# Pairwise bilinear interaction: embedding depth on the partitions, six large stores per tile of 256 rows, each input tile loaded in quarters

## The chip, the cores and the metric

The kernel runs on one core of one Trainium2 chip. The metric is the device time of one execution in microseconds, the median of several runs. The transpositions of arrays on the host, before and after the launch, are not in this time.

## What is computed

The input `x` has 4096 rows (the batch), 32 fields per row and 64 numbers per field, in float32. `W` is a 64 x 64 matrix. Every field is multiplied by `W`, and then, for each of the 496 pairs of fields i < j, the left field is multiplied element by element with the projected right field:

```python
vid = jnp.einsum('bfd,de->bfe', x, W)
idx_i, idx_j = jnp.triu_indices(32, k=1)
return x[:, idx_i, :] * vid[:, idx_j, :]        # (4096, 496, 64)
```

The pairs are ordered by i, then by j: field 0 has the first 31 pairs, field 1 the next 30, field 30 the last one. The output is 520 MB, the input 34 MB.

## The kernel before

The batch lies on the partitions: a tile is 128 rows, one row per partition, and there are 32 tiles. For each tile:

- **Load** (line 61): one DMA of 1 MB from the SP queue. There are three buffers. The tile's load is issued two tiles ahead (lines 64 and 76; `AHEAD = 2`), before the stores of the tile that is then worked on.
- **Transposes** (line 85): the projection contracts over the depth, so the depth must be on the partitions. TensorE transposes two fields at a time, 16 transposes of 128 x 128 per tile, four to a PSUM bank; ScalarE copies each bank to `xT` in SBUF (line 86).
- **Projection** (line 97): 31 small matmuls per tile, one for each field but field 0 (the profile counts two matmul instructions for each), with `xT` of one field as the stationary side and `W` as the moving side (64 columns). The even fields of the pairs lie on partitions 0 to 63, the odd ones on 64 to 127, so `W` is loaded twice (lines 68 and 69, from ScalarE's queue). ScalarE copies the products from PSUM to `vid` (line 106), two buffers.
- **Products** (line 117): VectorE has one instruction for each left field i. It multiplies field i, broadcast along the pairs, with fields i+1 to 31 of `vid`, and writes 31-i pairs (of 64 numbers) to an output tile.
- **Stores** (line 124): consecutive left fields are gathered until they hold at most 66 pairs (`CHUNK`); each such chunk is one store from the SP queue. There are nine stores per tile, of 0.9 to 2.1 MB, from six output buffers.

Waits between engines and DMAs are put in by the tile framework: a consumer waits for the producers of what it reads, and a writer of a buffer waits until its earlier users are through. The order on each engine's queue is that of the program, planned by the framework's scheduler, which may move an instruction by its priority. On SP stand only loads and stores: a store there waits for VectorE's products, and everything behind it on SP waits with it.

Line 142 of the profile's rows is where the kernel's core object is made, and line 151 is the launch; neither does work on the data.

Of the kernel before, what the change touches and what calls it, by code (L numbers as in the profile page):

```python
# [1 line left out]

# [5 lines left out]

F32 = mybir.dt.float32
ALU = mybir.AluOpType  # L10


def field_chunks(nf, most):
    """Consecutive left fields i whose pairs (i, j > i) make one store of at most `most` pairs."""
    chunks, cur, size = [], [], 0
    for i in range(nf - 1):
        n = nf - 1 - i
        if cur and size + n > most:
            chunks.append((cur, size))
            cur, size = [], 0  # L20
        cur.append(i)
        size += n
    chunks.append((cur, size))
    return chunks


@with_exitstack
def pairwise_bilinear_kernel(
    ctx: ExitStack,
    tc: tile.TileContext,  # L30
    x: bass.AP,
    w: bass.AP,
    out: bass.AP,
):
    nc = tc.nc
    P = 128
    B, F, D = x.shape
    NT = B // P
    # Two fields (2 * D = 128 columns) share one transpose; 4 transposes fill a
    # PSUM bank, and so do the products of 8 fields.  # L40
    TPB = 4
    GRP = 8
    NGRP = F // (2 * GRP)
    CHUNK = 66
    AHEAD = 2

    const = ctx.enter_context(tc.tile_pool(name="const", bufs=1))
    xpool = ctx.enter_context(tc.tile_pool(name="x", bufs=AHEAD + 1))
    tpool = ctx.enter_context(tc.tile_pool(name="xT", bufs=2))
    vpool = ctx.enter_context(tc.tile_pool(name="vid", bufs=2))  # L50
    opool = ctx.enter_context(tc.tile_pool(name="out", bufs=6))
    ps_t = ctx.enter_context(
        tc.tile_pool(name="ps_t", bufs=3, space=bass.MemoryType.PSUM)
    )
    ps_v = ctx.enter_context(
        tc.tile_pool(name="ps_v", bufs=2, space=bass.MemoryType.PSUM)
    )

    def load(t):
        xt = xpool.tile([P, F, D], F32, tag="x", name=f"x_{t}")  # L60
        nc.sync.dma_start(out=xt, in_=x[t * P : (t + 1) * P])
        return xt

    loaded = [load(t) for t in range(min(AHEAD, NT))]

    # W on both halves of the partitions, for the even and the odd field of a pair.
    w2 = const.tile([P, D], F32)
    nc.scalar.dma_start(out=w2[0:D, :], in_=w)
    nc.scalar.dma_start(out=w2[D : 2 * D, :], in_=w)
    ident = const.tile([P, P], F32)  # L70
    make_identity(nc, ident)

    chunks = field_chunks(F, CHUNK)
    for t in range(NT):
        if t + AHEAD < NT:
            loaded.append(load(t + AHEAD))
        xt = loaded[t]

        # xT[(parity, d), pair, b] = x[b, 2 * pair + parity, d]
        xT = tpool.tile([P, F // 2, P], F32, tag="xT", name=f"xT_{t}")  # L80
        for g in range(F // 2 // TPB):
            pt = ps_t.tile([P, TPB, P], F32, tag="pt", name=f"pt_{t}_{g}")
            for k in range(TPB):
                f = 2 * (g * TPB + k)
                nc.tensor.transpose(pt[:, k, :], xt[:, f : f + 2, :], ident)  # L85
            nc.scalar.copy(xT[:, g * TPB : (g + 1) * TPB, :], pt)  # L86

        # vid[b, j] = x[b, j] @ W. Field 0 is never the right one of a pair.
        vid = vpool.tile([P, F // 2, 2, D], F32, tag="vid", name=f"vid_{t}")
        for g in range(NGRP):  # L90
            pv = ps_v.tile([P, 2, GRP, D], F32, tag="pv", name=f"pv_{t}_{g}")
            for k in range(GRP):
                pair = g * GRP + k
                for h in range(2):
                    if pair == 0 and h == 0:
                        continue
                    nc.tensor.matmul(  # L97
                        pv[:, h, k, :],
                        lhsT=xT[h * D : (h + 1) * D, pair, :],
                        rhs=w2[h * D : (h + 1) * D, :],  # L100
                        start=True,
                        stop=True,
                    )
            for h in range(2):
                k0 = 1 if g == 0 and h == 0 else 0
                nc.scalar.copy(  # L106
                    vid[:, g * GRP + k0 : (g + 1) * GRP, h, :], pv[:, h, k0:, :]
                )
        vid = vid.rearrange("p g h e -> p (g h) e")

        start = 0
        for c, (fields, size) in enumerate(chunks):
            ot = opool.tile([P, CHUNK, D], F32, tag="o", name=f"o_{t}_{c}")
            at = 0
            for i in fields:
                n = F - 1 - i
                nc.vector.tensor_tensor(  # L117
                    ot[:, at : at + n, :],
                    xt[:, i : i + 1, :].to_broadcast([P, n, D]),
                    vid[:, i + 1 :, :],  # L120
                    ALU.mult,
                )
                at += n
            nc.sync.dma_start(
                out=out[t * P : (t + 1) * P, start : start + size, :],
                in_=ot[:, :size, :],
            )
            start += size


_INS = ["r_x", "L0_rec_W"]
_OUTS = [((4096, 496, 64), "float32")]


# [21 lines left out]
```

## Time and profile before

| | |
|---|---|
| median of 9 runs | 1331.4 us (1328.48 to 1336.02) |
| the profiled execution's own time | 1336.02 us |
| its span in the profile | 1334.2 us |
| bytes read from and written to HBM | 33.59 and 520.09 MB, 415 GB/s over the span |
| VectorE busy | 1142.1 us (86%), 992 instructions |
| TensorE busy | 257.6 us (19%), 2496 matmul and transpose instructions |
| ScalarE busy | 139.3 us (10%), 257 instructions |
| granted TensorE clock, mean | 0.566 |

A group's row in the profile reads: line, engine, operation, output <- inputs, shapes, how often; then the busy time in us and the mean duration of one in ns; then how long the engine stood idle just before these instructions, and what ended most of that idle time. The DMA row gives, for each of 40 equal slices of the span, the mean busy share of the 16 DMA engines in tenths; the row under it gives the GB/s that they moved. A row of DMA issues gives the operands, the queue (SPq is SyncE's), how often, the size, and the median time from issue to landing. The profile's chain is the work that ended last, followed back from the end to whatever released each step.

### The profile page before, as it was taken

The page shows a single profiled execution, that of the slowest core. Times are in us where ns is not written, and L with a number is a line of the kernel's source. Part 1 is how long each engine was busy: PE and PEld are TensorE (multiplying, and loading weights), DVE is VectorE, ACT ScalarE, POOL GpSimd, SP SyncE. Part 2 cuts the span into 40 slices and gives each one's busy share as a digit, 9 for nine tenths or more (in the row PEclk, how much of TensorE's full clock was granted, in tenths as well). Part 3 has the DMA queues.
Part 4 walks back from the last instruction along what each step waited for, and adds up shares of the span by engine and source line. Part 5 has one row for each costly group of instructions (what it writes and reads, how often), then busy time and mean ns, then how long its engine had stood idle before and what let it go on. Part 6 is the DMA issues. An engine that isn't in the chain of part 4 may idle for free.

```text
span 1334.2 us, 7305 instructions
## 1 busy us (share of the span) xinstructions
PE 257.6 (19%) x2496; PEld 244.5 (18%) x2496; DVE 1142.1 (86%) x992; ACT 139.3 (10%) x257; POOL 0.7 (0%) x6
## 2 busy tenths in 40 slices
PE   5012221222212332102222022220122311322000
PEld 5012221122211332102222022220122311322000
DVE  5999888888888888889888888888898888988893
ACT  3011101011010110101101011100111010110000
POOL 0000000000000000000000000000000000000000
PEclk9566665566655556556665566665666555566555
DMA  6999999999999999999999999999999999999996
GB/s 271 404 428 429 427 422 425 421 429 423 421 421 425 425 428 426 420 427 428 427 427 419 421 421 416 426 421 420 419 418 429 420 418 425 411 427 418 421 428 282
DMA packets 46277, 554.16 MB, mean 415 GB/s; under 512 B 5280, under 2 KB 5280, under 8 KB 9376
## 3 DMA queue, kind: packets, MB, share of 16 engines
q1 hardware_dynamic: 46080, 553.67, 98.8%
q8 instruction: 19, 0.31, 0.1%
q14 instruction: 18, 0.15, 0.0%
q10 hardware_dynamic: 160, 0.03, 0.0%
HBM read 33.59 MB, written 520.09 MB: 415 GB/s over the span
## 4 chain that ended last, share of the span: by engine, by line
DMA 75%; DVE 21%; issue 2%; PE 1%; DVEq 0%; ACT 0%
DMA out_dram<-o 75%; DVE o L117 21%; DMA x<-in_r_x_dram 0%; PE pv L97 0%; PE pt L85 0%; DVEq L117 0%; ACT vid L106 0%; DVEq L151 0%
## 5 line engine op out<-in xcount | busy, mean ns | idle before, releaser
L117 DVE TENSOR_TENSOR o<-x,vid 128x1984 f32<-128x1984 f32 (+30 forms) x992 | 1142.1, 1220 | 171.3 <-DMA out_dram<-o 156.8
L85 PE MATMUL pt<-ident,x 128*128 128x128 f32 x512 | 111.6, 408 | 970.4 <-DMA x<-in_r_x_dram 970.0
L85 PEld LDWEIGHTS pt<-ident,x 128*128 128x128 f32 x512 | 100.9, 220 | 974.4 <-issue 973.4
L86 ACT COPY xT<-pt 128x512 f32<-128x512 f32 x128 | 74.1, 588 | 711.4 <-PE pt L85 711.0
L97 PE MATMUL pv<-w,xT 64*128 64x64 f32 x1984 | 148.4, 311 | 0.0
L97 PEld LDWEIGHTS pv<-w,xT 64*128 64x128 f32 x1984 | 143.6, 224 | 8.9 <-issue 8.9
L106 ACT COPY vid<-pv 128x512 f32<-128x512 f32 (+1 forms) x128 | 64.2, 586 | 385.6 <-DVE o L117 381.4
L86 ACT ACT_TABLE_LOAD x1 | 1.3, 1283 | 2.0 <-issue 2.0
masks.py:199 POOL TENSOR_SCALAR_AFFINE_SELECT ident<-ident 128x128 f32<-128x128 f32 x1 | 0.3, 292 | 0.1
masks.py:197 POOL MEMSET ident<- 128x128 f32 x1 | 0.2, 204 | 0.3 <-POOLq L142 0.3
L142 POOL MEMSET const-bfloat16-1.0<- 128x1 bf16 x1 | 0.1, 101 | 0.0
L142 POOL MEMSET const-uint8-127<- 128x1 uint8 x1 | 0.1, 101 | 0.0
L142 POOL MEMSET const-float32-0.0<- 128x1 f32 x1 | 0.1, 98 | 0.2 <-issue 0.2
L142 POOL MEMSET const-float32-1.0<- 128x1 f32 x1 | 0.1, 98 | 0.0
## 6 DMA issues: line engine op xcount, KB each, us to landing
out_dram<-o SPq DMA_DIRECT2D x64, 1824.0 KB, 23.3
out_dram<-o SPq DMA_DIRECT2D x32, 2112.0 KB, 22.5
out_dram<-o SPq DMA_DIRECT2D x32, 2016.0 KB, 21.7
out_dram<-o SPq DMA_DIRECT2D x32, 1984.0 KB, 21.5
out_dram<-o SPq DMA_DIRECT2D x32, 1952.0 KB, 24.6
out_dram<-o SPq DMA_DIRECT2D x32, 1696.0 KB, 24.2
out_dram<-o SPq DMA_DIRECT2D x32, 1568.0 KB, 23.5
x<-in_r_x_dram SPq DMA_DIRECT2D x32, 1024.0 KB, 24.5
```

The source lines that it names most:

```text
L85: nc.tensor.transpose(pt[:, k, :], xt[:, f : f + 2, :], ident)
L86: nc.scalar.copy(xT[:, g * TPB : (g + 1) * TPB, :], pt)
L97: nc.tensor.matmul(pv[:, h, k, :], lhsT=xT[h * D : (h + 1) * D, pair, :], rhs=w2[h * D : (h + 1) * D, :], start=True, stop=True,)
L106: nc.scalar.copy(vid[:, g * GRP + k0 : (g + 1) * GRP, h, :], pv[:, h, k0:, :])
L117: nc.vector.tensor_tensor(ot[:, at : at + n, :], xt[:, i : i + 1, :].to_broadcast([P, n, D]), vid[:, i + 1 :, :], ALU.mult,)
L142: nc = _bacc.Bacc("TRN2", target_bir_lowering=False, num_devices=1)
```

## The change

The host hands the kernel another layout, and takes the output back in another. The batch is cut in two halves of 2048 rows. A tile is now 256 rows, 128 from each half, and there are 16 tiles. Partitions 0 to 63 hold the 64 depths of the first half's rows, partitions 64 to 127 those of the second half's; along the free dimension lie 32 fields x 128 rows. The output is laid out in the same way, 496 pairs x 128 rows per partition. In the kernel:

- The transposes, their copies and the identity go. A matmul now has `W` as its stationary side and four fields (512 columns) as its moving side, one for each half of the partitions: 16 matmuls per tile of 256 rows, in four groups of 8 fields, each group in two PSUM banks and followed by one copy of 1024 columns on ScalarE. Field 0 is projected too.
- A product instruction works on fields of 128 numbers instead of 64. Pairs are stored in slots of 83 (`SLOT`), six slots per tile, the last of 81; a left field that crosses a slot's end is cut in two instructions. There are three output buffers.
- SP's instructions are issued in the order in which the program writes them (`manual_schedule` for SP).
- Input buffers: two instead of three. Tile 0 is loaded in four quarters (8 fields each), the last fields first, then tile 1 in two halves; both at the start. The quarters of every later tile t+1 are issued on SP behind the second, third, fourth and fifth of the six stores of tile t, fields 0 to 7 first.
- Tile 0 is worked from its last pair backwards and stored in smaller pieces (four stores for the first slot, two for each other slot), and its groups are projected in reverse.

```diff
-    TPB = 4
     GRP = 8
-    NGRP = F // (2 * GRP)
-    CHUNK = 66
+    NGRP = F // GRP
+    BANK = 512 // C
+    SLOT = 83
     AHEAD = 2
+    PIECES = 4
...
+    ctx.enter_context(tc.manual_schedule(engines={mybir.EngineType.SP}))
...
-    xpool = ctx.enter_context(tc.tile_pool(name="x", bufs=AHEAD + 1))
-    tpool = ctx.enter_context(tc.tile_pool(name="xT", bufs=2))
+    xpool = ctx.enter_context(tc.tile_pool(name="x", bufs=AHEAD))
     vpool = ctx.enter_context(tc.tile_pool(name="vid", bufs=2))
-    opool = ctx.enter_context(tc.tile_pool(name="out", bufs=6))
+    opool = ctx.enter_context(tc.tile_pool(name="out", bufs=3))
...
+    def load(t, lo, hi):
+        if t not in xs:
+            xs[t] = xpool.tile([P, F, C], F32, tag="x", name=f"x_{t}")
+        nc.sync.dma_start(out=xs[t][:, lo:hi, :], in_=x[t][:, lo:hi, :])
...
+        vid = vpool.tile([P, F, C], F32, tag="vid", name=f"vid_{t}")
+        for g in order:
+            pv = psum.tile([P, GRP, C], F32, tag="pv", name=f"pv_{t}_{g}")
+            for b in range(0, GRP, BANK):
+                f = g * GRP + b
                 for h in range(2):
+                    half = slice(h * D, (h + 1) * D)
                     nc.tensor.matmul(
+                        pv[half, b : b + BANK, :],
+                        lhsT=w2[half, :],
+                        rhs=xs[t][half, f : f + BANK, :],
                         start=True,
                         stop=True,
                     )
+            nc.scalar.copy(vid[:, g * GRP : (g + 1) * GRP, :], pv)
...
+    def products(t, vid, ot, base, a, b, backwards=False):
+        fields = [i for i in range(F - 1) if off[i] < b and off[i + 1] > a]
+        for i in reversed(fields) if backwards else fields:
+            s, e = max(a, off[i]), min(b, off[i + 1])
+            j = i + 1 + s - off[i]
+            nc.vector.tensor_tensor(
+                ot[:, s - base : e - base, :],
+                xs[t][:, i : i + 1, :].to_broadcast([P, e - s, C]),
+                vid[:, j : j + e - s, :],
+                ALU.mult,
             )
...
+    def store(t, ot, base, a, b):
+        nc.sync.dma_start(out=out[t][:, a:b, :], in_=ot[:, a - base : b - base, :])
+
+    for g in reversed(range(NGRP)):
+        load(0, g * GRP, (g + 1) * GRP)
+    load(1, F // 2, F)
+    load(1, 0, F // 2)
+
+    for t in range(NT):
+        vid = project(t, reversed(range(NGRP)) if t == 0 else range(NGRP))
+        bases = list(range(0, NP, SLOT))
+        if t == 0:
+            ends = [NP, off[27], off[24], off[21], bases[-1]]
+            for n, base in enumerate(reversed(bases)):
+                top = min(base + SLOT, NP)
+                if n:
+                    ends = [top, (base + top) // 2, base]
+                ot = opool.tile([P, SLOT, C], F32, tag="o", name=f"o_{t}_{n}")
+                for b, a in zip(ends, ends[1:]):
+                    products(t, vid, ot, base, a, b, backwards=True)
+                    store(t, ot, base, a, b)
+        else:
+            for n, base in enumerate(bases):
+                top = min(base + SLOT, NP)
+                ot = opool.tile([P, SLOT, C], F32, tag="o", name=f"o_{t}_{n}")
+                products(t, vid, ot, base, base, top)
+                store(t, ot, base, base, top)
+                if 1 <= n <= PIECES and t + 1 < NT and t + 1 not in (0, 1):
+                    load(t + 1, (n - 1) * F // PIECES, n * F // PIECES)
```

`off[i]` is the number of pairs ahead of left field i. `C` is 128, `NP` is 496.

## The prediction

> **What bounds the kernel now.** I read the page from its DMA row downwards, then the chain, then the product, matmul and issue rows, and last the trace at the two ends.
>
> ```profile
> span 1334.2 us, 7305 instructions
> ...
> DMA  6999999999999999999999999999999999999996
> GB/s 271 404 428 429 427 422 425 421 429 423 421 421 425 425 428 426 420 427 428 427 427 419 421 421 416 426 421 420 419 418 429 420 418 425 411 427 418 421 428 282
> ...
> q1 hardware_dynamic: 46080, 553.67, 98.8%
> ...
> DMA out_dram<-o 75%; DVE o L117 21%; DMA x<-in_r_x_dram 0%; PE pv L97 0%; PE pt L85 0%; DVEq L117 0%; ACT vid L106 0%; DVEq L151 0%
> ...
> L117 DVE TENSOR_TENSOR o<-x,vid 128x1984 f32<-128x1984 f32 (+30 forms) x992 | 1142.1, 1220 | 171.3 <-DMA out_dram<-o 156.8
> ...
> out_dram<-o SPq DMA_DIRECT2D x32, 1984.0 KB, 21.5
> out_dram<-o SPq DMA_DIRECT2D x32, 1952.0 KB, 24.6
> ...
> x<-in_r_x_dram SPq DMA_DIRECT2D x32, 1024.0 KB, 24.5
> ```
>
> The DMA row stands at 9 in 38 of 40 slices, and the chain is mostly stores: the kernel is bound by 553.67 MB of transfers, nearly all stores. VectorE is busy 1142.1 us and waits 156.8 us for output buffers, so it is only 14% short of being the bound itself. The load row matters most below: a load takes 24.5 us to land, because five or six stores stand ahead of it on the same queue. It costs nothing now, as it is issued two tiles (82 us) ahead.
>
> ```profile
> L117 DVE TENSOR_TENSOR o<-x,vid 128x1984 f32<-128x1984 f32 x32 | 71.2, 2225 | 35.3 <-DMA out_dram<-o 20.8 <-ACT vid L106 14.5
> ...
> L117 DVE TENSOR_TENSOR o<-x,vid 128x64 f32<-128x64 f32 x32 | 7.0, 218 | 0.0
> ```
>
> Those are two product rows by shape (busy us, mean ns). Next four lines of the timeline (start, us, engine, line): the matmuls of three tiles' projections, 62 instructions each for 31 products, and one load's issue in mid-run, which took 23.9 us to land.
>
> ```profile
> 9.44 3.90 PE L97 MATMUL pv<-w,xT 64*128 64x64 f32 x62
> ...
> 358.19 3.78 PE L97 MATMUL pv<-w,xT 64*128 64x64 f32 x62
> ...
> 441.31 7.09 PE L97 MATMUL pv<-w,xT 64*128 64x64 f32 x62
> ...
> 619.53 1.14 SPq L61 DMA_DIRECT2D x<-in_r_x_dram  x1
> ```
>
> Finer windows show first bytes at 1.5 us, full rate from 2.6 to 10.0 us (loads), nothing until 19.4 us (first store), and last bytes at 1332.7 us, 1.5 us before the span's end. **Pace:** 553.67 MB / (1332.7 - 2.6 - 9.4) = 419, say 420 GB/s.
>
> **What the Trainium skill says.** *DMA: Bandwidth & Descriptors*, "Queues, rings and completion order": each DMA engine consumes descriptors in ring order, one ring per engine for SP. The trace agrees: loads land after 24.5 us, stores after 21.5 to 24.6. *VectorE: DVE Perf Modes*, "The perf-mode tier table": fp32 tensor_tensor runs only at 1x. The trace agrees: (2225-218)/(1984-64) = 1.045 ns an element. *FP8 and Floating Point Precision*, "TensorE Precision Notes": an fp32 matmul makes four passes. The trace agrees: the burst at granted clock 0.50 (7.09 us) takes 229 ns a product, 274 cycles of 1.2 GHz for 64 columns. *TensorEngine Tiling (Array Packing)*, "Key Properties": tiles on different rows of the array work in parallel. No run here shows it: 274 cycles fit halves that take turns (4 x 64), but also parallel halves held up by their weights (128 columns, two instructions).
>
> **The change, part by part.** Bytes stay: a tile of 256 rows is 32.51 MB of stores and 2.10 MB of loads. A slot of 83 pairs stores 5.439 MB (12.95 us at 420), the last of 81 pairs 5.308 MB (12.64), a load quarter 0.524 MB (1.25).
>
> *VectorE.* Elements stay at 1,015,808 per partition: 1061.5 us at 1.045; the other 80.6 us of busy time are 81 ns for each of 992 instructions. After: 36 instructions a tile (31 fields, five cut at slot ends), so 63488 x 1.045 + 36 x 81 ns = 69.3 us a tile. The first slot (3 instructions) takes 11.35 us. Saving 416 instructions (34 us) brings nothing by itself: the transfers cover it.
>
> *Transposes and their copies* (111.6 us PE, 74.1 us ACT) go. They lay beside the stores in all tiles but the first: worth nothing there.
>
> *Start.* VectorE begins at 14.48 us now: load, transposes (3.65 us), matmuls, copies. After, it needs a quarter load, W (5.7 us from issue at 0.74, so 6.5), 4 matmuls (2.0 at the full clock that the trace shows here) and a copy (1.05): 9.7 us.
>
> *Matmuls.* Four of 512 columns per group of 8 fields. A matmul is 4 x 512 cycles. At half clock, halves in parallel, a group takes 2 x 2048 / 1.2 GHz + 0.2 = 3.6 us, an estimate from the two pages and the burst at clock 0.50. Bounds: 1.9 (full clock) and 7.0 (half clock, halves in turn). I take half clock, because PE stands idle some 14 us between quarters, and the parallel halves of the tiling page: the weights are loaded for only 64 columns now, so they hold up less. **Copy:** 588 ns for 512 columns, 0.83-1.1 ns a column more: 1.05 us for 1024.
>
> *Loads: the step that decides.* Before, a tile is loaded two tiles ahead. After, tile t+1's quarters are issued behind stores 2 to 5 of tile t's six, on the same SP queue. SP waits for each store's products first. Every pair's right field is above its left, so every first-slot product of t+1 needs the last quarter (fields 24-31). The quarter's own issue (1.1 us of SP's time in the load's row, four a tile) hides in the 11 us between two stores; it passes no other queue. Its wait for the x buffer (two now, three before) is over: tile t-1's products ended before the first store of t. So there is a loop that closes once a tile:
> - first slot's products 11.35, issue to first byte 0.7 (18.80 to 19.5 for the first store);
> - then the queue, back to back: 5 stores + 4 quarters = 29.29 MB / 420 = 69.74;
> - last byte to release 0.75 (the first store: 6.2 us to landing less 0.7 and 4.76 of transfer), PE start 0.13, matmuls 3.6, copy 1.05, VectorE start 0.1.
>
> Sum **87.4 us**, where the transfers alone need 82.4. Only the sixth store (12.64 us) lies behind the last quarter and covers its way back to a new store: 0.75+0.13+3.6+1.05+0.1+11.35+0.7 = 17.7. DMA idles 5.0 us a tile. VectorE's products plus latency alone (12.8) exceed the cover. Deeper buffers don't help: three slots of 12.95 never hold VectorE back within a tile (slot 3 would start 34 us in, the first store is through after 26).
>
> *Sum.* Tile 0, stored in pieces from the back: VectorE ends its first slot at 21.6 (81 x 128 x 1.045 + 13 x 81 ns), the next half slot at 27.5; from 28.2 on transfers bound it: 27.20 MB more, to 92.95. VectorE is through at 79.8. Tile 1's first store is ready at 91.85, no gap. Tile 2 starts at 92.95 + 69.74 + 5.63 = 168.3; tile 15 after 13 loops at 1304.8; its stores end 11.35 + 0.7 + 77.4 later: 1394.3, +1.5 = **span 1395.8**. Outside the span lie 1336.0 - 1334.2 = 1.8: 1397.6 against the profiled execution's 1336.0, +4.6%. The runs' median, 1331.4, is 0.34% below that execution; so 1393.
>
> *Descriptors.* 46080 packets are 320 DMAs x (128 rows + 16). After: 166 DMAs, rows of 42 KB. If all time in excess of the DMA page's fabric ceiling of 435 GB/s ("Specifications") goes with packets, 48 us fall to 25 and the pace becomes 427; if none does, it stays 420. The longer row pitch of the output could also slow it (lowest slice: 411). I take 420.
>
> **Rivals.**
> (a) *The loop, but a better pace:* 427 GB/s gives a loop of 86.3 and, by the same sum, 1374. For: half the packets. Against: at the start, loads in rows of 8 KB ran no slower (427 to 434 GB/s) than stores in rows of up to 17 KB.
> (b) *The matmul's halves take turns:* 7.0 for 3.6, 14 tiles: +48, 1440. For: 274 cycles. Against: the tiling page.
> (c) *No gap, faster:* the last quarter is not held up behind the fifth store. It decides at 11.9 us: if quarter, matmuls and copy are done within the last slot's products, the queue never empties; then 92.95 + 15 x 77.4 + 14 x 4.99 + 1.5 + 1.8 = 1327, as a median 1323. For: the quarters are small and 16 engines serve the queue. Against: 24.5 us of the load row.
> (d) *VectorE becomes the bound:* 16 x 69.3 = 1109; nothing speaks for it.
>
> **How the numbers follow.** Loop as priced 0.46, (a) 0.18, (b) 0.22: slower, 0.86. (c) 0.12: faster. 0.02 that pace and waits cancel. Some 0.2% is what a measurement of this kernel can tell from no change. Range: low 1350 = (a) with full-clock matmuls (-25), high 1445 = (b) and a little for its rounding; (c) and 0.06 beyond are left out.
>
> **What would show it.** Right: 14 waits of VectorE of some 18 us for ACT's copy, at the starts of tiles 2 to 15; DMA row below 9 about once in 87 us; last quarter landing some 20 us or more after issue; first slot's three products 11.35 us. Wrong: quarters landing within 12 us, VectorE waiting for stores instead, or a mid-run rate well above 430 GB/s.

## The result, and the profile after

The changed kernel takes **1415.1 us** in the median of 10 runs (1412.5 to 1418.5), the kernel before 1330.5 us in 32 runs. The ratio is **1.063** (95% interval 1.061 to 1.065): slower, by 6.3%, where 4.6% were forecast (1393 us, range 1350 to 1445). The profiled execution has a span of 1411.5 us, where the prediction's sum had 1395.8.

The page of the changed kernel, the lines that answer to those shown of before:

```profile
span 1411.5 us, 2185 instructions
...
DVE  6999397694986949859498594985949959499594
...
DMA  8999989899797997989989899798998989989799
GB/s 338 429 428 416 409 344 429 345 412 431 327 432 341 415 430 332 431 353 408 429 336 429 359 409 430 334 426 344 414 430 348 412 357 411 430 352 409 341 443 401
...
q1 hardware_dynamic: 23904, 553.66, 92.9%
...
DVE o L88 57%; DMA x<-in_r_x_dram 26%; PE pv L72 4%; ACT vid L79 1%; SPq L96 0%; DMA w<-in_L_rec_W_dram 0%; DVEq L154 0%
...
L88 DVE TENSOR_TENSOR o<-x,vid 128x1408 f32<-128x1408 f32 (+15 forms) x581 | 1099.4, 1973 | 292.0 <-ACT vid L79 292.0
...
x<-in_r_x_dram SPq DMA_DIRECT2D x60, 512.0 KB, 21.0
```

The bytes are the same, but the DMA row no longer stands at 9: every two or three slices it falls to 7 or 8, and the GB/s under it from 430 to about 340. The chain has changed hands. Before, three quarters of it were stores; now it is products, then loads, then matmuls and copies, in turn: a chain that goes round. VectorE no longer waits for output buffers at all; all its 292.0 us of waiting are for ScalarE's copies into `vid`.

One turn of the chain, in order of time (start us, duration us, what), from the issue of the fifth store to the next tile's first product:

```profile
494.44 0.33 SPq L96
...
494.82 26.17 DMA x<-in_r_x_dram
...
521.12 3.69 PE pv L72 x8
...
524.84 1.02 ACT vid L79
...
525.88 0.04 DVE o L88
```

SP issues the fifth store, then at once the last quarter. That quarter takes 26.17 us to land, since it stands behind what is left of the fourth store, the third quarter and the whole fifth store. Then come the four matmuls (eight instructions, 3.69 us), the copy and the release of VectorE. In the windows that follow (columns: stretch and its length, busy time of PE, PEld, DVE, ACT and POOL, granted clock, DMA share, GB/s) the queue runs dry. A window counts a row of a transfer where it starts, and a row of these stores takes about 1.6 us:

```profile
526.00:530.00 4.00, 0.00 (x0) 0.00 (x0) 4.00 (x1) 0.00 (x0) 0.00 (x0) 0.50 1.01 435
530.00:532.00 2.00, 0.00 (x0) 0.00 (x0) 2.00 (x2) 0.00 (x0) 0.00 (x0) 0.50 0.39 166
532.00:537.90 5.90, 0.00 (x0) 0.00 (x0) 5.90 (x3) 0.00 (x0) 0.00 (x0) 0.50 0.00 0
538.00:542.00 4.00, 0.00 (x0) 0.00 (x0) 4.00 (x3) 0.00 (x0) 0.00 (x0) 0.50 1.19 510
```

The sixth store, issued at 506.1, lands 27.1 us later, at about 533. VectorE works all the time on the next tile's first slot, but the store of that slot is issued only at 537.3, and its first bytes move at 538. For some 5 us nothing is on the way, as much as the prediction's sum had. VectorE's timeline shows the period (start, length of the run of instructions, first shape, how many, and in brackets the wait before it):

```profile
171.06 68.70 DVE L88 TENSOR_TENSOR o<-x,vid 128x3968 f32<-128x3968 f32 x36 [21.91 <-ACT vid L79]
259.83 68.70 DVE L88 TENSOR_TENSOR o<-x,vid 128x3968 f32<-128x3968 f32 x36 [20.07 <-ACT vid L79]
...
1322.71 68.70 DVE L88 TENSOR_TENSOR o<-x,vid 128x3968 f32<-128x3968 f32 x36 [20.20 <-ACT vid L79]
```

There are 14 such waits of about 20 us, at tiles 2 to 15. A tile takes (1322.71 - 171.06)/13 = **88.6 us**; forecast were 87.4.

### The profile page after: what moved, and what is told of

Read it like the earlier page. It is cut to its first block, busy times and chain, and to the rows that moved or that the text cites. A ratio compares the mean times of both kernels' runs of the same rounds, so it can differ in the third digit from the quotient of the medians.

```text
span 1411.5 us, 2185 instructions
## 1 busy us (share of the span) xinstructions
PE 221.9 (16%) x512; PEld 56.8 (4%) x512; DVE 1099.4 (78%) x581; ACT 66.1 (5%) x65; POOL 0.2 (0%) x4
## 4 chain that ended last, share of the span: by engine, by line
DVE 57%; DMA 27%; issue 9%; PE 4%; ACT 1%; SPq 0%; DVEq 0%
DVE o L88 57%; DMA x<-in_r_x_dram 26%; PE pv L72 4%; ACT vid L79 1%; SPq L96 0%; DMA w<-in_L_rec_W_dram 0%; DVEq L154 0%
## 5 line engine op out<-in xcount | busy, mean ns | idle before, releaser
L88 DVE TENSOR_TENSOR o<-x,vid 128x1408 f32<-128x1408 f32 (+15 forms) x581 | 1099.4, 1973 | 292.0 <-ACT vid L79 292.0
L72 PE MATMUL pv<-x,w 64*64 64x512 f32 x512 | 221.9, 1012 | 1099.8 <-DMA x<-in_r_x_dram 1094.4
L79 ACT COPY vid<-pv 128x1024 f32<-128x1024 f32 x64 | 64.8, 1012 | 1254.7 <-PE pv L72 1254.7
L72 PEld LDWEIGHTS pv<-x,w 64*64 64x64 f32 x512 | 56.8, 206 | 1263.1 <-issue 1252.3
```

What stands on the lines that cost most here:

```text
L72: nc.tensor.matmul(pv[half, b : b + BANK, :], lhsT=w2[half, :], rhs=xs[t][half, f : f + BANK, :], start=True, stop=True,)
L79: nc.scalar.copy(vid[:, g * GRP : (g + 1) * GRP, :], pv)
L88: nc.vector.tensor_tensor(ot[:, s - base : e - base, :], xs[t][:, i : i + 1, :].to_broadcast([P, e - s, C]), vid[:, j : j + e - s, :], ALU ...
```

## The experiments

**Theory:** the last quarter's place behind the fifth store closes a loop once a tile, with one store as cover, and the queue runs dry in each turn. **Rivals:** (1) the transfers themselves are slower in the new layout; (2) three output buffers are too few for stores of 5.4 MB; (3) TensorE's work is off the path and doesn't matter. Ratios are to the kernel before, run on the same chip beside each.

### Quarters one store earlier

```diff
-                if 1 <= n <= PIECES and t + 1 < NT and t + 1 not in (0, 1):
-                    load(t + 1, (n - 1) * F // PIECES, n * F // PIECES)
+                if n < PIECES and t + 1 < NT and t + 1 not in (0, 1):
+                    load(t + 1, n * F // PIECES, (n + 1) * F // PIECES)
```

> The four quarters of tile t+1 stand behind stores 1 to 4 of tile t instead of 2 to 5; nothing else differs. Theory (the once-a-tile loop: last quarter behind the fifth store, only the sixth store as cover): two stores (some 25 us) now cover a way of about 17.5 us, the queue never empties, VectorE's waits for ScalarE's copy at tile starts go, and a tile takes what its transfers take. In the trace of the changed kernel six stores take 74.7 us at 435 GB/s and a quarter some 2.05 us, so 82.9 us a tile instead of 88.6: span about 1332 us, ratio to the kernel before 1.00 (0.99 to 1.01). Rival 1 (the changed kernel is slow because its transfers are slow: other row sizes and another row pitch): the time stays near 1411. Rival 2 (three output buffers are too few for such large stores): also near 1411, with VectorE waiting for stores.

Measured: 1341.3 us, ratio 1.007 (1.005 to 1.009). Moving four loads by one store takes 74 us off. The page of this run:

```profile
DMA  8999999999999999999999999999999999999997
...
L88 DVE TENSOR_TENSOR o<-x,vid 128x1408 f32<-128x1408 f32 (+15 forms) x581 | 1101.7, 1971 | 212.7 <-ACT vid L79 135.2
...
410.00:420.00 10.00, 0.00 (x0) 0.00 (x0) 10.00 (x4) 0.00 (x0) 0.00 (x0) 0.54 0.79 341
```

The DMA row is back at 9 in all slices but the first and the last, and a tile takes 83.7 us (82.9 expected). VectorE still waits 135 us for ScalarE's copy, 9 us at the start of each tile, but that is within what VectorE has to spare in a tile (83.7 us, of which it works 68.7). Rivals 1 and 2 fall as explanations of the gap.

The queue is not quite full, though: the last line above is a window of this run at the turn of a tile, with a DMA share of 0.79. The trace has the landing of a transfer on each of the 16 DMA engines, and in this run three of them are some 7 us behind. Of the store issued at 430.98, for instance, 13 engines are done by 449.1, the last three at 453.4, 455.0 and 456.3. So 12 or 13 engines run dry for about 2 us before a tile's first store, while three or four always have work; the slowest set the pace of 83.7 us. In the changed kernel, whose queue runs empty in each tile, all 16 are done with a store at nearly the same time (the fifth one of the turn above: 518.0 to 519.3). Why three fall behind, these runs do not show.

### Quarters one store later

```diff
-                if 1 <= n <= PIECES and t + 1 < NT and t + 1 not in (0, 1):
-                    load(t + 1, (n - 1) * F // PIECES, n * F // PIECES)
+                if 2 <= n <= PIECES + 1 and t + 1 < NT and t + 1 not in (0, 1):
+                    load(t + 1, (n - 2) * F // PIECES, (n - 1) * F // PIECES)
```

> The quarters stand behind stores 3 to 6: no store is left behind the last quarter. Loop theory: a tile takes 11.3 + 0.8 (first slot's products, first byte) + 74.7 + 8.2 (six stores, four quarters) + 0.75 + 4.9 (release, matmuls, copy) = 100.7 us instead of 88.6: the span grows by 14 x 12.1 = 169 us to about 1580, ratio 1.19. Rivals 1 and 2 (slow transfers, too few output buffers): no change from the changed kernel, ratio 1.063.

Measured: 1580.2 us, ratio 1.185 (1.181 to 1.188), a span of 1574.7. VectorE's timeline of this run:

```profile
182.50 68.69 DVE L88 TENSOR_TENSOR o<-x,vid 128x3968 f32<-128x3968 f32 x36 [33.10 <-ACT vid L79]
...
1485.86 68.69 DVE L88 TENSOR_TENSOR o<-x,vid 128x3968 f32<-128x3968 f32 x36 [31.70 <-ACT vid L79]
```

A tile takes 100.3 us (expected 100.7). With one, two and no stores behind the last quarter the same bytes take 1415, 1341 and 1580 us.

### The last group's matmuls twice

```diff
-            for b in range(0, GRP, BANK):
+            for b in list(range(0, GRP, BANK)) * (2 if t > 1 and g == NGRP - 1 else 1):
```

> The changed kernel, but from tile 2 on the four matmuls of the last group of fields (24 to 31) are done twice, into the same place. Loop theory: TensorE's time for this group (3.7 us) is on the loop, so 14 x 3.7 = 51 us are added: span about 1463, ratio 1.10. If TensorE is beside the path (it is busy for 16% of the span), the time stays at ratio 1.063.

Measured: 1446.6 us, ratio 1.085 (1.082 to 1.088), a span of 1444.1: 33 us more, where 51 were expected. Two groups in this run's timeline:

```profile
514.82 3.68 PE L72 MATMUL pv<-x,w 64*64 64x512 f32 x8 [10.81 <-DMA x<-in_r_x_dram]
528.83 6.36 PE L72 MATMUL pv<-x,w 64*64 64x512 f32 x16 [10.33 <-DMA x<-in_r_x_dram]
```

Twice the work took 2.68 us more here, not 3.68: the longer burst ended faster (granted clock 0.50 in its first 5 us, 0.81 in its last 1.4). The 14 doubled bursts took 5.0 to 6.6 us, 5.9 in the mean, so 2.2 us more each: 14 x 2.2 = 31, nearly all of the 33. So the place on the path is confirmed, and rival 3 falls: an engine that is busy for 16% of the span is on the path with its last 3.7 us of every tile. The expectation's error was to charge the repetition at the pace of the first half.

### The whole load behind the first store, and four quarters together

```diff
-                if 1 <= n <= PIECES and t + 1 < NT and t + 1 not in (0, 1):
-                    load(t + 1, (n - 1) * F // PIECES, n * F // PIECES)
+                if n == 0 and t + 1 < NT and t + 1 not in (0, 1):
+                    load(t + 1, 0, F)                                      # first run
+                    for k in range(PIECES):                                # second run, in place of it
+                        load(t + 1, k * F // PIECES, (k + 1) * F // PIECES)
```

> Tile t+1 is loaded by one DMA of 2 MB behind store 1 of tile t. The loop predicts no idle queue, as with the quarters one store earlier. What this tells apart is the price of a quarter: in the changed kernel's trace four quarters seem to take some 8.2 us in the queue, 3.4 us more than their bytes at 435 GB/s. If each change from stores to a load and back costs (about 0.85 us), one load a tile instead of four saves 3 x 0.85 us x 14 tiles = 36 us against the quarters one store earlier: about 1296. If rows of 4 KB instead of 16 KB are what costs, the same gain is expected, so this run alone doesn't part these two. If neither costs, both runs come out alike.

> The same four quarter loads (rows of 4 KB) as in the changed kernel, but all four behind store 1, back to back. The runs before gave 1341 us for four quarters behind four stores and 1311 us for one load of 2 MB behind one store: a tile takes 83.75 and 81.2 us, that is about 0.87 us more than the bytes' time for every stretch of loads. If the change between stores and a load is what costs, four quarters together are one stretch: about 1311 us. If the rows of 4 KB are what costs, 1341 as with the quarters apart.

Measured: 1310.9 us, ratio 0.983 (0.980 to 0.985), for the whole load; 1301.6 us, ratio **0.978** (0.976 to 0.980), for the four quarters together. The latter is the fastest kernel of this study. VectorE's timeline of it, in one tile:

```profile
152.18 11.36 DVE L88 TENSOR_TENSOR o<-x,vid 128x3968 f32<-128x3968 f32 x3 [0.84 <-DMA out_dram<-o]
164.62 11.43 DVE L88 TENSOR_TENSOR o<-x,vid 128x896 f32<-128x896 f32 x4 [1.07 <-DMA out_dram<-o]
...
207.25 11.57 DVE L88 TENSOR_TENSOR o<-x,vid 128x1408 f32<-128x1408 f32 x6 [6.33 <-DMA out_dram<-o]
219.76 11.78 DVE L88 TENSOR_TENSOR o<-x,vid 128x384 f32<-128x384 f32 x13 [0.94 <-DMA out_dram<-o]
232.33 11.36 DVE L88 TENSOR_TENSOR o<-x,vid 128x3968 f32<-128x3968 f32 x3 [0.79 <-DMA out_dram<-o]
```

VectorE now waits for output buffers about 1 us a slot, the sign that the transfers are the bound, and 6.3 us where the loads are in the queue. A tile takes 80.5 us, with the quarters apart 83.7. The same four DMAs, with the same rows of 4 KB, cost 3.2 us less a tile when they stand together: it is the stretches of loads between stores that cost, about 1 us for each of the three that go away, and not the rows of 4 KB. That is the cost on the slowest engines. Added up over all 16, the pages have the transfers at 97.7% of 1340.6 us with the quarters apart and at 99.5% of 1299.4 us together, 17 us more and not 40; nearly all the rest is time in which most engines had run dry while the slow ones worked. What happens inside the DMA engines at such a change, these runs do not show.

### The first slot stored in thirds, then all slots

```diff
-                products(t, vid, ot, base, base, top)
-                store(t, ot, base, base, top)
+                for a, b in ((0, 28), (28, 56), (56, top)) if n == 0 else ((base, top),):       # first run
+                for a, b in ((base, base + 28), (base + 28, base + 56), (base + 56, top)):     # second run
+                    products(t, vid, ot, base, a, b)
+                    store(t, ot, base, a, b)
```

> The changed kernel with its quarters where they are, but from tile 1 on the first slot's store is cut into three (28, 28 and 27 pairs, each stored when its products are done). Loop theory: the products of the first slot are on the loop with their 11.35 us; with 28 pairs the first new store is ready after 3.8 us, so the way from the last quarter's last byte to a new store is 0.75 + 4.9 + 3.8 + 0.8 = 10.2 us, less than the 12.2 us of the sixth store: no empty queue, 83.75 us a tile as with the quarters one store earlier, about 1343 us, ratio 1.01. If the moment at which the load is issued is the trouble for another reason (the matmuls, the buffers), the time stays near 1415.

Measured: 1398.9 us, ratio 1.050 (1.048 to 1.053). That is 16 us less than the changed kernel and not the 70 expected. The windows of one tile (its first products start at 608.89) tell why:

```profile
622.00:626.00 4.00, 0.00 (x0) 0.00 (x0) 4.00 (x2) 0.00 (x0) 0.00 (x0) 0.50 1.03 436
626.00:630.00 4.00, 0.00 (x0) 0.00 (x0) 4.00 (x2) 0.00 (x0) 0.00 (x0) 0.50 0.08 35
630.00:634.00 4.00, 0.00 (x0) 0.00 (x0) 4.00 (x3) 0.00 (x0) 0.00 (x0) 0.50 0.40 170
```

The queue no longer runs dry before the first slot's store, but 17 us into the tile, before the second slot's: VectorE gains only about 1 us on the transfers in a slot (11.4 against 12.5), so a store that goes out early doesn't bring the next one forward. The gap had moved. The expectation had followed the loop only as far as the first store. If that is so, all slots must be cut:

> The changed kernel, quarters where they are, but from tile 1 on every slot's store is cut into three (28, 28 and 27 pairs), not the first slot's alone. With the first slot alone cut, the queue ran empty after its three pieces instead, since the second slot's products take 11.4 us and only 12.5 us of stores were ahead: the time fell by 16 us, not by 70. If that is the reason, cutting all of them keeps the queue fed: VectorE makes 28 pairs in 3.8 us, their store takes 4.2, and the first slot's 11.35 us on the loop become 3.8. The loop is then 3.8 + 0.8 + 63.2 (27.2 MB at 430) + 8.2 to 9 + 5.65 = 82 us, below the 84.9 us that a tile's transfers take (81.6 in the run with rows of 14 KB and quarters together, and 3.3 more for quarters apart): about 1316 + 14 x 3.3 = 1362 us, ratio 1.023 (1.015 to 1.035). If the first slot's products are not what the loop consists of, the time stays above 1395.

Measured: 1351.7 us, ratio 1.016 (1.013 to 1.018); the page's DMA row is at 9 in all slices but the first. A tile takes 84.2 us (84.9 expected), although VectorE still waits 14 to 15 us for ScalarE's copy at each start. So the gap has two cures: earlier loads, or smaller stores throughout. Both leave most DMA engines idle for some 2 us a tile, since the slowest are behind the others here too.

### Quarters on ScalarE's queue

```diff
-                    load(t + 1, (n - 1) * F // PIECES, n * F // PIECES)
+                    lo, hi = (n - 1) * F // PIECES, n * F // PIECES
+                    if t + 1 not in xs:
+                        xs[t + 1] = xpool.tile([P, F, C], F32, tag="x", name=f"x_{t + 1}")
+                    nc.scalar.copy(xs[t + 1][:, lo, 0:1], ot[:, top - base - 1, 0:1])
+                    nc.scalar.dma_start(out=xs[t + 1][:, lo:hi, :], in_=x[t + 1][:, lo:hi, :])
```

> The quarters are issued from ScalarE's queue instead of SP's, at the same moments as in the changed kernel: a one-column copy on ScalarE from the last pair of the slot into the quarter holds each load back until the slot's products are done (the column is then overwritten by the load). Loop theory in the form that the place in SP's ring is what counts: on a ring of its own a quarter takes turns with the stores on each DMA engine, 8 rows against 8 rows of a store, so it lands some 13 us after issue instead of 26; the last quarter, the matmuls and the copy are then through about 76 us after the tile's start, which is within the time of its transfers, and the time falls to that of the quarters one store earlier, about 1341, or somewhat more if the alternation costs. If it is the moment of issue that counts and not the ring (a load waits for all older stores whatever its queue), nothing changes: 1415, ratio 1.063.

Measured: 1571.0 us, ratio 1.181 (1.178 to 1.183). The run did not do what it was meant to. Its timeline:

```profile
621.67 3.68 PE L72 MATMUL pv<-x,w 64*64 64x512 f32 x8 [40.66 <-DMA x<-in_r_x_dram]
...
625.38 1.01 ACT L79 COPY vid<-pv 128x1024 f32<-128x1024 f32 x1 [20.36 <-PE pv L72]
626.29 0.19 ACT L128 COPY x<-o 128x1 f32<-128x1 f32 x1
626.51 0.33 ACTq L129 DMA_DIRECT2D x<-in_r_x_dram  x1
```

On ScalarE's queue the copy of one group of `vid` had been planned ahead of the next quarter's issue. So each quarter was issued only when the one before had landed and been projected, and the last of this tile went out at 672.8 us, 9 us before the next tile's first product. Here the DMA that was moved to a working engine's queue waited for that engine's own waits too. With ScalarE's instructions in the order of the program, too:

```diff
-    ctx.enter_context(tc.manual_schedule(engines={mybir.EngineType.SP}))
+    ctx.enter_context(tc.manual_schedule(engines={mybir.EngineType.SP, mybir.EngineType.Activation}))
```

> The quarters on ScalarE's queue again, with the same one-column copies that hold each back to the moment of the changed kernel, but ScalarE's instructions in the order of the program too: in the run before, the copies of one group stood ahead of the next quarter's issue on ScalarE, and so each quarter waited for the projection of the one before it. There a quarter landed 16.6 to 18.4 us after issue beside stores, against 26 in the changed kernel. So: last quarter issued 57.4 us after the tile's start, landed at about 75, projected and copied at 80: less than the 83.75 us of a tile's transfers, so no or nearly no empty queue and about 1340 us (1320 to 1360), ratio 1.01. If a ring of its own doesn't help, 1415; if alternation by rows slows both streams, between.

Measured: 1382.7 us, ratio 1.038 (1.036 to 1.041): between the two expectations. The last quarter's way, in this run's timeline:

```profile
656.64 0.33 ACTq L129 DMA_DIRECT2D x<-in_r_x_dram  x1
...
680.51 3.67 PE L72 MATMUL pv<-x,w 64*64 64x512 f32 x8 [10.18 <-DMA x<-in_r_x_dram]
```

The four quarters of this tile reach TensorE 16.7, 19.0, 21.5 and 23.9 us after issue. On a queue of its own the last one saves some 2.5 us against the 26.3 of the changed kernel, and a tile takes 86.0 us. The trace's records of single rows show why it saves no more. The 128 rows of a quarter begin 16 at a time, as many as there are DMA engines, every 1.7 us. That is what one row of a store (42 KB, 1.57 us) and one row of the quarter (4 KB, 0.16 us) take together. So the two queues take turns row by row, although the one's rows are ten times the other's, and a quarter needs 13.8 us, as long as the whole store beside it: the last one lands at 680.4, the store issued just before it at 680.2. A new quarter is issued every 11.4 us, so each waits 2.4 us longer than the one before it behind the quarters on its own queue. The turns are those of the expectation of the run before (8 rows against 8 rows); what both expectations left out is the quarters' own queue.

### Late loads in the old layout

In the kernel before, `loaded = [load(0)]` stands for the two first loads, SP's order is as written, and in the loop:

```diff
-        if t + AHEAD < NT:
-            loaded.append(load(t + AHEAD))
...
             start += size
+            if c == 5 and t + 1 < NT:
+                loaded.append(load(t + 1))
```

> The kernel before, in its old layout with transposes, three input and six output buffers, but each tile's load is issued behind store 6 of 9 of the tile ahead of it, with stores 7 to 9 (153 pairs, 5.0 MB, 11.7 us) left as cover; SP's order is as written. If the loop is made by where the load stands and not by the new layout or by the number of buffers, a gap appears here as well: way from the load's last byte to a new store = 0.9 (release and start) + 3.65 (transposes) + 3.9 to 7.1 (matmuls) + 1.1 (copies) + 4.3 (first chunk's products) + 0.7 = 14.6 to 17.8 us, less 11.7: 3 to 6 us in each of 31 tiles, so 1330 + 90 to 190 = 1420 to 1520 us, ratio 1.07 to 1.14. If the layout or the buffers are to blame in the changed kernel, the time stays at 1330.

Measured: 1509.2 us, ratio 1.134 (1.131 to 1.137). VectorE's timeline of two tiles:

```profile
623.36 35.29 DVE L116 TENSOR_TENSOR o<-x,vid 128x1984 f32<-128x1984 f32 x31 [13.48 <-ACT vid L105]
669.30 30.93 DVE L116 TENSOR_TENSOR o<-x,vid 128x1984 f32<-128x1984 f32 x21 [10.66 <-ACT vid L105]
```

The same waits, 369 us in all, now in the old kernel: neither the layout, nor the missing transposes, nor the number or size of the output buffers is needed for the gap. A load that stands too near the end of the tile before makes it.

### The pace of the stores: two loads only, and smaller rows

The first run is the kernel before with two input buffers, and after the two first loads:

```diff
-        if t + AHEAD < NT:
-            loaded.append(load(t + AHEAD))
-        xt = loaded[t]
+        xt = loaded[t % AHEAD]
```

> The kernel before, but only tiles 0 and 1 are loaded and all later tiles use their data again: 30 of the 32 loads of 1 MB (31.5 MB) are left out, the stores are all there. It parts two reasons for the old kernel's pace of 420 GB/s. If the stores' rows of at most 17 KB are slower than the 42 KB rows (435 GB/s in the changed kernel's last tile, which has no loads beside it), stores alone still run at about 420: 520.1 MB take 1238 us and the time is about 1263. If it is the changes between stores and loads that cost (0.87 us for each), stores alone run at 435: 1196 us and about 1220 in all.

Measured: 1249.2 us, ratio 0.939 (0.937 to 0.942), nearer to 1263 than to 1220. The page's rate is 422 to 429 GB/s in all slices but the first and the last: in the old layout stores alone run at 425. The 31.5 MB left out account for 80 us, 2.7 us a load, hardly more than their bytes at 425 (2.5). So the change between stores and loads is nearly free there, and what the old kernel's pace lacks to 435 is the stores' own.

The second run is the kernel with four quarters together, with every slot from tile 1 on stored in thirds, as shown above:

> The four quarters together behind store 1 (1302 us in the run before), but from tile 1 on each slot's store is cut in three: rows of 14 KB per partition instead of 42 KB, 18 stores a tile. The old layout's stores alone ran at 425 GB/s with rows of at most 17 KB; the changed kernel's last tile, 42 KB rows without loads, at 433 to 436. If the size of the rows is the reason, the pace falls by 2.2%: 15 tiles x 80.5 x 0.022 = 27 us more, about 1328 us. If it is the layout (row pitch, halves of the batch), nothing changes: 1302.

Measured: 1316.2 us, ratio 0.989 (0.987 to 0.991). Smaller rows cost 15 us, half of the 27 expected: 81.6 us a tile instead of 80.5. The other half of the distance between 425 and 435 GB/s belongs to something else in the layout, and stays open.

## Why the prediction was right, and where its terms were off

**The mechanism held.** The last quarter's place was the step that decides, the loop closed as described, and 14 waits of VectorE for ScalarE's copy appeared (20 us instead of 18). Its terms, in the loop that starts at 437.40:

| term | forecast us | measured us |
|---|---|---|
| products of the first slot | 11.35 | 11.36 |
| 5 stores and 4 quarters in the queue | 69.74 | about 70.7 |
| TensorE start, last group's matmuls | 3.7 | 3.83 |
| copy | 1.05 | 1.02 |
| whole loop | 87.4 | 88.6 (mean of 13) |
| of it, nothing on the way | 5.0 | about 5 |

The measured queue is the quarter's landing (520.99) less the start (437.40), the first slot's products, 0.8 to the first byte and 0.75 to the release.

**The term that was mis-sized is the queue,** by 1 us net, and it hides two errors; that they nearly cancel is luck. The stores were priced at 420 GB/s. In the last tile, which has no loads beside it, they go from 1334 to 1409 us: 32.5 MB at 433 GB/s, and in the windows before a tile's first quarter at 435:

```profile
449.00:474.00 25.00, 0.00 (x0) 0.00 (x0) 25.00 (x11) 0.00 (x0) 0.00 (x0) 0.50 1.04 435
474.00:497.00 23.00, 7.35 (x16) 1.68 (x16) 23.00 (x13) 1.76 (x2) 0.00 (x0) 0.59 0.97 400
```

The second line is a stretch with two quarters in it. At 435 five stores take 62.5 us and not 64.75. The quarters were priced by their bytes, 5.0 us for four. They take the rest, 8.2 us. The loop waits for the slowest of the 16 DMA engines: in the same time the others had already moved some 0.4 MB of the sixth store (0.9 us), so a part of the 8.2 is that the engines don't end together. The old kernel's mean pace had held both, but with 32 loads among 288 stores; the new kernel has 62 among 104, and each costs more beyond its bytes. 13 loops x 1.17 us make 15.2 of the 15.7 us by which the span was missed.

**The start** was 1.8 us late (VectorE at 11.5, not 9.7): TensorE waited 5.4 us for W's first half and 1.1 for its second, and the first group took 5.1 us to be through. Tile 2 began at 171.1, not 168.3. **The end** gave 2.2 us back: the last tile's stores ran faster than 420.

**The rivals.** (a), a better pace, was half right: the stores had it, the quarters took it away. (b) fell: a group takes 3.69 us at granted clock 0.50, against estimates of 3.6 for halves side by side and 7.0 for halves in turn. So the matmul's halves work at the same time, as the Trainium skill says of tiles of the array (*TensorEngine Tiling (Array Packing)*, "Key Properties"). The kernel before couldn't show this. Half clock was a choice between the two that the kernel before showed; these bursts have it (221.9 us for 64 groups, 3.5 each). How long a cycle is at that clock, no run shows by itself: the comparison is of durations. (c) fell: the last quarter lands 26 us after issue, not within 11.9. Even on a queue of its own it takes 24. VectorE as the bound, (d): 1099.4 us busy against 1109 forecast, and never the bound.

**What was missed in the prediction's view of the loop:** it looked at one gap before one store. The better sum is VectorE's slack. A tile with quarters apart takes 83.7 us when the slowest DMA engines always have work; VectorE works 68.7. It may wait 15.0 us and no more. It waits 20, and the 5 us are the loss, wherever in the tile they show. The run with the first slot in thirds taught this: its gap moved to the second slot's store.

**What the change can bring.** With the loads placed well the changed kernel takes 1302 us, 2.2% less than before. About half of these 29 us goes with the rows of 42 KB (1316 us with rows of 14 KB); the shorter start (VectorE at 11.5 us, not 14.5) is a small part, and the rest was not taken apart. The quarters' places take back 74 us as the queue runs dry, and their being apart another 40 (1341 to 1302).

## What to carry to other kernels

In these runs a load on the same queue as the stores landed when everything issued before it was through. So count the work issued *behind* it, up to the moment its data is needed, as its cover, and compare that with the whole way from its landing to the next store. When an engine is only slightly faster than the transfers, each wait beyond its slack per tile is lost, and a store sent earlier only moves the gap. Cutting a load into pieces spread among stores doesn't hide it: the last piece decides, and here every extra stretch of loads cost about 1 us. And a DMA share near 1 over a long slice doesn't say that every engine is busy: look at the turn of a tile in short windows.

## What the runs showed of the hardware that was not expected

- Loads between stores cost more than their bytes with rows of 42 KB in the stores: about 2.1 us for 0.52 MB up to the landing on the slowest DMA engine (1.2 by the bytes at 435 GB/s), and 83.7 us a tile for four stretches against 80.5 for one. In the old layout, 30 loads of 1 MB cost 2.7 us each against 2.5 by their bytes.
- Stores in rows of 14 KB instead of 42 KB took 1.1% longer in all (1316.2 against 1301.6 us).
- The 16 DMA engines did not stay abreast on a queue that never ran dry: with the quarters one store earlier, three of them were some 7 us behind the other 13.
- Two queues took turns row by row: a load of 0.52 MB in rows of 4 KB on ScalarE's queue, beside stores of 5.4 MB in rows of 42 KB on SP's, moved 16 rows every 1.7 us and needed 13.8 us, as long as a store. With the loads ahead of it, it landed 16.6 to 23.7 us after its issue.
- Matmuls of 64 x 64 on the two halves of the array's rows and columns ran at the same time: four fp32 matmuls of 512 columns in 3.69 us at granted clock 0.50, against an estimate of 7.0 for halves in turn.
